# Self edges as a copied half tile, two extra gathers per half block, one weight table per block

## The chip, the cores and the metric

The kernel runs on one core of a Trainium2 chip. The metric is the device time of one execution in microseconds; the times shown are medians over runs. A profile is one execution recorded by the hardware, with its own time.

## The reference

A graph of 3327 nodes (padded to 3328 = 26 x 128) with 128 features, and a dense 3327 x 3327 matrix of edge weights in which about 2% of the entries are not zero; the diagonal always has its edge (the self edge). Two layers run one after the other:

```python
# layer 0: four heads of graph attention
h  = relu(layernorm(x))
x1, x2 = h @ w1[k], h @ w2[k]                        # per head k
s  = leaky_relu(x1[:, None] + x2[None, :], 0.01) @ a[k]
s  = exp(8 * tanh(s / 8)) * adj                      # zero where there is no edge
out_k = leaky_relu((s / s.sum(-1)) @ h @ Wlin[k].T, 0.01)
x  = x + concat(out_k) @ w
# layer 1: graph convolution with symmetric normalisation
h  = relu(layernorm(x)); A = adj + I; d = A.sum(1) ** -0.5
x  = x + relu((d[:, None] * A * d[None, :]) @ (h @ W.T + b))
```

## The kernel before

**Sparse scores.** A score is needed only where there is an edge. The kernel goes through the 26 blocks of 128 destination rows, each in two halves of 64 rows. It makes a list of the edges of each row and gathers, by indirect DMA, one table row per edge: 128 edges (one per partition) per gather. A table row holds the neighbour's normalised features (128), four score terms, ones, its x2 of all four heads (512), and in front of these (FEAT = 64 columns) the edge weights between this neighbour and the 64 rows of the half. There are two tables in HBM, one for each half; their weight columns are written anew by `weights` (L569 to L574) for every block and half, from AT_d, the transposed adjacency that `tables_step` (L352 to L362) writes.

**Lists.** `prep` (from L345) is a generator whose steps are dealt out among the other work. VectorE (DVE) turns the adjacency rows of a block into codes (L402), takes the largest eight codes of each short segment (L406), then selects, for each half of the columns, 32 entries per row by four rounds of "largest eight, remove them" over 136 candidates (L433 to L438), and 40 more from all 272 (the loop at L456 to L462). The first 64 fill a regular pattern of slots: 32 gathers per half, in four tiles `g` of eight gathers. What is left over, the extras, is packed by a small matrix product into OVT = 3 gathers per half, the tile `ge`. The self edge is an edge like any other in this list.

**Per half.** `groups` are nine steps m: two for each tile g and one, m = 8, for ge. `stage_z` (L577 to L603) turns the gathered x2 of four times 128 edges and four heads into PSUM by transposing on TensorE (L588). For g tiles DVE takes the maximum with -x1, which is laid out by slots (L600); for ge, x1 is added by a product with the incidence matrix `oi` (L591), and ScalarE (ACT) takes the relu (L597). `stage_r` (L605 to L612) multiplies with the attention vector: `sel` places the result of head h in rows of 32h to 32h + 31, four heads side by side in TensorE (L611). `finish` (from L615) turns the scores, takes tanh and exp, multiplies with the edge weights and aggregates (L659 for g, L677 for ge). `close` ends a half and, after the second, the block.

**Order and queues.** The order of instructions is written out by hand: `slot` is called several times per group and runs the pending ends, `advance` (which runs as many steps of `prep` of the next blocks as the time that has passed asks for), `fetch` (which queues the gathers of a tile as soon as its buffer is free: four buffers g, one ge) and `trickle` (which issues them). Gathers are issued by GpSimd (POOL); loads of the adjacency, weights, xn_d and hTb by SyncE (SP); AT_d by ACT. Each queue is in order.

**End.** Layer 1 is a matrix product over the transposed adjacency, read back from AT_d in strips of four blocks: a part in advance during the last block (`begin`, L874), the rest at the end (`layer1`, L938). `columns` (L831 to L841) cuts these reads.

Of the kernel before, what the change touches and what calls it, by code (L numbers as in the profile page):

```python
# [63 lines left out]
ROW = 720  # L64
COLS = 709
WIDE = 712
FEAT = 64
PROJ = 197
# [161 lines left out]
def _sparse_layers(tc, nc, x, adj, w1, w2, a, wlin, w, gw, gb, gb_sb, gwT, x_sb, dinv, flag, ident, out):  # L230
# [24 lines left out]
    with ExitStack() as l0:  # L255
        res = l0.enter_context(tc.tile_pool(name="res", bufs=1))
        dram = l0.enter_context(tc.tile_pool(name="dram", bufs=1, space=bass.MemoryType.DRAM))
        tables = [dram.tile([NP + 1, ROW], F32, name=f"table{k}") for k in range(2)]
# [5 lines left out]
        AT_d = dram.tile([NS * NP, 4 * P], F32, name="AT_d")  # L264
# [3 lines left out]
        sel = res.tile([P, H, 63], F32, name="sel")  # L268
        p_all = res.tile([P, NB, 2 * H], F32, name="p_all")
        code = res.tile([P, NP], mybir.dt.uint16, name="code")  # L270
        epos = res.tile([P, 2 * OVT], F32, name="epos")
# [10 lines left out]
        pat = l0.enter_context(tc.tile_pool(name="pat", bufs=4))  # L282
# [12 lines left out]
        nc.gpsimd.iota(epos, [[-P, 2 * OVT]], base=2 * NP, channel_multiplier=-1, allow_small_or_imprecise_dtypes=True)  # L295

        nc.gpsimd.iota(first, [[0, 2], [16, 4], [0, 2]], base=0, channel_multiplier=0, allow_small_or_imprecise_dtypes=True)
# [4 lines left out]
        nc.vector.tensor_scalar(hoff[:, :1], rowid, float(HALF), float(OVT * P), op0=OP.is_ge, op1=OP.mult)  # L302
        nc.vector.tensor_scalar(hoff[:, 1:], hoff[:, :1], float(OVT * P), None, op0=OP.add)
        nc.vector.tensor_scalar(rowid, hoff[:, :1], -HALF / (OVT * P), rowid, op0=OP.mult, op1=OP.add)
# [10 lines left out]
        nc.gpsimd.affine_select(lower[:, HALF:], lower[:, HALF:], [[0, HALF]], OP.is_ge, 0.0, base=-HALF, channel_multiplier=1)  # L315

# [28 lines left out]
        def prep(b, k):  # L345

            adjb = blks[b].adjb
            csum = pb.tile([P, 4], F32, name="csum")
# [3 lines left out]
            def tables_step(j0):  # L352
                n = min(4, NB - j0)
                pt = ps_tr.tile([P, 4, P], F32, name="tr")
                for q in range(n):
# [3 lines left out]
                at0 = (b // 4) * NP  # L359
                eng = nc.scalar if b else nc.sync  # L360
                eng.dma_start(AT_d[at0 + j0 * P:at0 + (j0 + n) * P, b % 4 * P:b % 4 * P + P].rearrange("(b p) c -> p b c", p=P),
                                  at[:, :n, :])  # L362
# [34 lines left out]
            for sgm in range(64):  # L397
                if sgm % 32 == 0:
                    codes = pa.tile([P, 2, part], mybir.dt.uint16, name="codes")
                    for i in range(2):  # L400
                        c0 = (sgm // 16 + i) * part
                        nc.vector.scalar_tensor_tensor(codes[:, i], adjb[:, c0:c0 + part], 0.0, code[:, c0:c0 + part],  # L402
                                                       op0=OP.not_equal, op1=OP.mult, accum_out=csum[:, sgm // 16 + i:sgm // 16 + i + 1])
                        yield
# [25 lines left out]
            lists = pb.tile([P, 64 + 46], F32, name="lists")  # L430
            k.lists = lists
            for c in range(2):
                for r in range(SLOTS // 8):  # L433
                    top = lists[:, SLOTS * c + 8 * r:SLOTS * c + 8 * r + 8]
                    nc.vector.max(top, cand[:, c, :SOME])
                    yield
                    nc.vector.match_replace(out=cand[:, c, :SOME], in_to_replace=top, in_values=cand[:, c, :SOME], imm_value=0.0)
                    yield  # L438
# [16 lines left out]
            flat = cand[:, :, :SOME]  # L455
            for r in range(EXTRA // 8):  # L456
                top = lists[:, 64 + 8 * r:64 + 8 * r + 8]
                nc.vector.max(top, flat)
                yield
                if r < EXTRA // 8 - 1:  # L460
                    nc.vector.match_replace(out=flat, in_to_replace=top, in_values=flat, imm_value=0.0)
                yield  # L462
# [12 lines left out]
            nc.scalar.copy(ext[:, 42:42 + H], p_all[:, b, H:])  # L475
            yield
# [12 lines left out]
            nc.vector.tensor_reduce(miss, csum, AX.X, OP.add)  # L489
# [5 lines left out]
            oi = pb.tile([P, 2 * OVT * P], F32, name="oi")  # L495
            nc.vector.tensor_scalar(oi, code[:, :2 * OVT * P], ext[:, 40:41], None, op0=OP.is_le)
            yield
            nc.vector.scalar_tensor_tensor(oi, code[:, :2 * OVT * P], end, oi, op0=OP.is_gt, op1=OP.mult)
# [6 lines left out]
            for t in range(2 * OVT):  # L505
                nc.tensor.matmul(ex_ps[:, t, :], oi[:, t * P:(t + 1) * P], ext, start=True, stop=True)
# [4 lines left out]
            rel = pb.tile([P, 2 * OVT], F32, name="rel")  # L511
            nc.vector.tensor_sub(rel, epos, ex[:, :, 40])
            big = [P, 2 * OVT, EXTRA]
            hit = pb.tile(big, F32, name="lq", bufs=1)
            nc.vector.tensor_tensor(hit, rel[:, :, None].to_broadcast(big), code[:, None, :EXTRA].to_broadcast(big), OP.is_equal)
            yield
            nc.vector.tensor_mul(hit, hit, ex[:, :, :EXTRA])
            hits = pb.tile([P, 2 * OVT], F32, name="hits")
            nc.vector.tensor_reduce(hits, hit, AX.X, OP.add)
            idxo = pb.tile([P, 2, OVT], mybir.dt.int32, name="idxo")  # L520
            nc.vector.tensor_scalar(idxo.rearrange("p c t -> p (c t)"), hits, -float(ROW), float(NP * ROW), op0=OP.mult, op1=OP.add)
# [30 lines left out]
        def gather(b, hb, w):  # L552

            k = blks[b]
            tab = tables[hb].rearrange("r (c u) -> (r c) u", u=1)
            if w == NW:
                g, n, at = pe_.tile([P, OVT, WIDE], F32, name="ge"), OVT, k.idxo[:, hb]
# [47 lines left out]
        def stage_r(k, hb, m, rs):  # L605
            n = 4 * P if m < 8 else OVT * P
            at = m % 2
            if at == 0:
                k.s = ps_s.tile([P, BANK], F32, name="s")
# [698 lines left out]
```

## Time and profile before

| | us |
|---|---|
| median of 3 runs | 2529.61 (2529.4 to 2537.58) |
| span of the profiled execution | 2534.6 |
| TensorE busy (modelled) | 2282.7 (90%) |
| VectorE busy | 2030.0 (80%) |
| ScalarE busy | 705.3 (28%) |
| GpSimd busy | 1792.0 (71%) |

The profiled execution took 2534.6 us from its first to its last instruction, 5 us more than the median of the runs. Issuing a DMA doesn't count as busy on SP and ACT; on POOL an indirect DMA does[...]. The mean granted TensorE clock is 0.979. The DMA engines are shown at 9 tenths or more in all slices but the last. A group's line reads: source line, engine, operation, output<-inputs by the program's names, shapes, count | busy us, mean ns of one | idle time of the engine before it, and who ended it.

### The profile page before, as it was taken

The page shows a single profiled execution, that of the slowest core. Times are in us where ns is not written, and L with a number is a line of the kernel's source. Part 1 is how long each engine was busy: PE and PEld are TensorE (multiplying, and loading weights), DVE is VectorE, ACT ScalarE, POOL GpSimd, SP SyncE. Part 2 cuts the span into 40 slices and gives each one's busy share as a digit, 9 for nine tenths or more (in the row PEclk, how much of TensorE's full clock was granted, in tenths as well). Part 3 has the DMA queues.
Part 4 walks back from the last instruction along what each step waited for, and adds up shares of the span by engine and source line. Part 5 has one row for each costly group of instructions (what it writes and reads, how often), then busy time and mean ns, then how long its engine had stood idle before and what let it go on. Part 6 is the DMA issues. An engine that isn't in the chain of part 4 may idle for free.

```text
span 2534.6 us, 51985 instructions
## 1 busy us (share of the span) xinstructions
PE 2282.7 (90%) x19410; PEld 1590.3 (63%) x19410; DVE 2030.0 (80%) x6260; ACT 705.3 (28%) x1651; POOL 1792.0 (71%) x1873
## 2 busy tenths in 40 slices
PE   6689999989988998999999999999999899999898
PEld 3466666666666666666666666666666666675553
DVE  7588988788887888888889888987988888795443
ACT  4122233223223222322322332232232223222110
POOL 3577777777777777777777777777777777777620
PEclk9699999999999999999999999999999999999999
DMA  9999999999999999999999999999999999999995
GB/s 298 389 333 334 332 357 317 329 352 334 315 338 343 319 327 358 324 328 344 339 316 340 355 314 338 348 334 321 343 344 317 324 361 314 332 323 343 328 333 196
DMA packets 460758, 838.58 MB, mean 331 GB/s; under 512 B 209098, under 2 KB 318164, under 8 KB 457172
## 3 DMA queue, kind: packets, MB, share of 16 engines
q0 software_dynamic: 145600, 640.34, 71.1%
q1 hardware_dynamic: 219396, 140.96, 19.1%
q10 hardware_dynamic: 95504, 53.88, 6.9%
q8 instruction: 156, 2.56, 0.4%
q14 instruction: 102, 0.84, 0.1%
HBM read 765.93 MB, written 113.42 MB: 347 GB/s over the span
## 4 chain that ended last, share of the span: by engine, by line
PE 36%; DVE 22%; DMA 20%; POOL 12%; issue 8%; ACT 0%; SPq 0%; DVEq 0%; POOLq 0%; ACTq 0%
DMA g<-table,idx 12%; POOL g L563 11%; DVE r L600 10%; PE z L588 10%; PE s L611 6%; DMA ge<-table,idxo 3%; PE z L591 3%; DMA AT_d<-at 2%; PE z L938 2%; DVE cand L406 2%; PE tr L628 2%; PE ag L659 2%; PE tr L371 1%; POOL ge L563 1%; DVE codes L402 1%
## 5 line engine op out<-in xcount | busy, mean ns | idle before, releaser
L563 POOL DMA_INDIRECT g<-table,idx x1664 | 1613.9, 970 | 568.4 <-issue 450.7
L588 PE MATMUL z<-ident,g 128*128 128x128 f32 x6656 | 929.9, 279 | 143.5 <-DVE r L600 106.2
L600 DVE TENSOR_TENSOR r<-z,x1n 128x1024 f32<-128x1024 f32 x832 | 1009.4, 1215 | 55.8 <-PE z L588 54.0
L588 PEld LDWEIGHTS z<-ident,g 128*128 128x128 f32 x6656 | 748.7, 142 | 361.7 <-DVE r L600 219.6
L611 PE MATMUL s<-r,sel 128*32 128x512 f32 (+1 forms) x3744 | 491.8, 598 | 0.7 <-ACT ssb L619 0.7
L619 ACT COPY ssb<-s 128x512 f32<-128x512 f32 x260 | 147.0, 565 | 533.9 <-PE s L611 531.4
L631 DVE TENSOR_TENSOR sc<-tr,g 128x32 f32<-128x32 f32 x208 | 38.4, 185 | 303.4 <-PE tr L628 303.4
L406 DVE MAX8 cand<-codes 128x8 f32<-128x52 uint16 x1664 | 214.9, 203 | 0.0
L563 POOL DMA_INDIRECT ge<-table,idxo x156 | 155.2, 995 | 49.0 <-issue 33.5
L639 ACT ACTIVATE th<-sc 128x32 f32<-128x32 f32 x260 | 58.3, 224 | 418.4 <-DVE sc L634 417.7
L591 PE MATMUL z<-oi,x1b 128*128 128x384 f32 x416 | 172.2, 496 | 0.0
L659 PEld LDWEIGHTS ag<-g,wt 128*32 128x32 f32 x3328 | 99.4, 110 | 115.4 <-issue 101.7
L358 ACT COPY at<-tr 128x512 f32<-128x512 f32 (+1 forms) x175 | 97.2, 555 | 215.9 <-PE tr L356 206.3
L628 PE MATMUL tr<-ident,ssb 128*128 128x128 f32 x988 | 152.6, 275 | 3.0 <-ACT at L358 2.7
L611 PEld LDWEIGHTS s<-r,sel 128*32 128x32 f32 x3744 | 73.9, 108 | 110.8 <-issue 86.6
L588 PEld LDWEIGHTS z<-ident,ge 128*128 128x128 f32 x624 | 80.7, 145 | 97.0 <-issue 27.7
L597 ACT ACTIVATE r<-z 128x768 f32<-128x768 f32 x104 | 84.4, 811 | 200.4 <-PE z L591 200.4
L659 PE MATMUL ag<-g,wt 128*32 128x133 f32 x3328 | 134.0, 279 | 0.0
L588 PE MATMUL z<-ident,ge 128*128 128x128 f32 x624 | 111.5, 282 | 23.3 <-DMA ge<-table,idxo 20.0
L356 PE MATMUL tr<-ident,adjb 128*128 128x128 f32 x676 | 107.8, 282 | 22.6 <-DMA adjb<-in_adj_dram 13.5
L628 PEld LDWEIGHTS tr<-ident,ssb 128*128 128x128 f32 x988 | 114.8, 141 | 11.1 <-ACT ssb L619 7.9
L402 DVE SCALAR_TENSOR_TENSOR codes<-adjb,code 128x832 uint16<-128x832 f32 x104 | 102.2, 1019 | 12.6 <-DMA adjb<-in_adj_dram 12.6
(188 smaller groups left out, 2347.4 us busy)
## 6 DMA issues: line engine op xcount, KB each, us to landing
adjb<-in_adj_dram SPq DMA_DIRECT2D x26, 1664.0 KB, 9.8
table<-AT_d SPq DMA_DIRECT2D x52, 832.0 KB, 17.0
AT_d<-at ACTq DMA_DIRECT2D x150, 256.0 KB, 5.7
g<-table,idx POOLq DMA_INDIRECT x1664
table<-img SPq DMA_DIRECT2D x12, 1312.0 KB, 4.9
adjb<-AT_d SPq DMA_DIRECT2D x18, 512.0 KB
g<-AT_d SPq DMA_DIRECT2D x7, 1024.0 KB
g<-AT_d ACTq DMA_DIRECT2D x5, 1024.0 KB, 11.0
```

What stands on the lines that cost most here:

```text
L356: nc.tensor.transpose(pt[:, q, :], adjb[:, (j0 + q) * P:(j0 + q + 1) * P], ident)
L358: nc.scalar.copy(at[:, :n, :], pt[:, :n, :])
L402: nc.vector.scalar_tensor_tensor(codes[:, i], adjb[:, c0:c0 + part], 0.0, code[:, c0:c0 + part], op0=OP.not_equal, op1=OP.mult, accum_out= ...
L406: nc.vector.max(cand[:, c, 8:].rearrange("p (r s) -> p r s", s=32)[:, :, sgm % 32], codes.rearrange("p a b -> p (a b)")[:, sgm % 32 * SEG: ...
L563: return nc.gpsimd.indirect_dma_start(out=g[:, t, lo:COLS], out_offset=None, in_=tab, in_offset=bass.IndirectOffsetOnAxis(ap=at[:, t:t + 1 ...
L588: nc.tensor.matmul(z[:, i, q * P:(q + 1) * P], g[:, m % 2 * 4 + q, PROJ + h * D:PROJ + (h + 1) * D], ident, is_transpose=True, start=(q == ...
L591: nc.tensor.matmul(z[:, i, :n], k.x1b[:, h * D:(h + 1) * D], k.oi[:, hb * n:(hb + 1) * n], start=False, stop=True, skip_group_check=True)
L600: nc.vector.tensor_tensor(r.rearrange("p h (i s) -> p h i s", s=16), z.rearrange("p h (i s) -> p h i s", s=16), k.x1n[:, 2 * hp:2 * hp + 2 ...
L611: nc.tensor.matmul(k.s[32 * h:32 * h + 32, :n], sel[:, h, 31 - at:63 - at], rs[h // 2][:, h % 2, :n], start=(at == 0), stop=(at == 1 or m ...
L619: nc.scalar.copy(ssb[:, :nk * P], s[:, :nk * P])
L628: nc.tensor.transpose(pt[:, q, :], ssb[:, q * P:(q + 1) * P], ident)
L659: nc.tensor.matmul(ag[32 * cg:32 * cg + 32, u, :WORK], wt[:, t].rearrange("p h q -> p (h q)"), g[:, t, FEAT:FEAT + WORK], start=(w == 0 an ...
```

## The change

Six things go together:

- The self edge is taken out of the codes: after L402, two DVE operations with the identity subtract the diagonal's code, and its sum is kept for the check that no edge is lost.
- The tile ge gets its self edges as a third, half-filled tile: 64 rows of the table copied by SP (the half's own rows, 64 partitions), beside FOUND = 2 gathered tiles instead of OVT = 3. ge becomes one lasting tile. For these 64 columns x1 comes by the maximum with x1n on DVE instead of the product with oi, which shrinks to two tiles; transposes and aggregation of this tile use 64 rows.
- Selection: all eight rounds of the first 64 entries go over both column halves' candidates (272) instead of four rounds for each (136).
- The table: rows are [64 weights | 648 body | 64 weights], 776 columns instead of 720; the second half's weights stand behind the body. The two tables alternate by blocks instead of by halves, and `weights` writes both halves' 128 columns at once, for the next block. A gather of the first half reads weights and body, one of the second body and weights.
- AT_d is laid out by blocks instead of by strips of four blocks. A strip is read back in one DMA for each block of it, in pieces of 128 columns instead of 512.
- The score matmul takes 2 columns of sel for each head instead of 32, into one lasting PSUM tile set to zero once; buffers `at` go from 4 to 3.

```diff
-ROW = 720
-COLS = 709
+FOUND = 2
+FEAT = 64
+BODY = 648
+ROW = FEAT + BODY + FEAT
+PROJ = 133
+COLS = 645
...
-        pat = l0.enter_context(tc.tile_pool(name="pat", bufs=4))
+        pat = l0.enter_context(tc.tile_pool(name="pat", bufs=3))
...
+                        lo, hi = max(c0, b * P), min(c0 + part, (b + 1) * P)
+                        if lo < hi:
+                            diag = pb.tile([P, P], F32, name="lq", bufs=1)[:, :hi - lo]
+                            mine = codes[:, i, lo - c0:hi - c0]
+                            nc.vector.scalar_tensor_tensor(diag, mine, -1.0, ident[:, lo - b * P:hi - b * P], op0=OP.mult, op1=OP.mult,
+                                                           accum_out=csum[:, sums[0]:sums[0] + 1])
+                            nc.vector.tensor_tensor(mine, mine, diag, OP.add)
+                            sums[0] += 1
...
-            for c in range(2):
-                for r in range(SLOTS // 8):
-                    top = lists[:, SLOTS * c + 8 * r:SLOTS * c + 8 * r + 8]
-                    nc.vector.max(top, cand[:, c, :SOME])
-                    yield
-                    nc.vector.match_replace(out=cand[:, c, :SOME], in_to_replace=top, in_values=cand[:, c, :SOME], imm_value=0.0)
-                    yield
+            flat = cand[:, :, :SOME]
+            def select(r):
+                top = lists[:, 8 * r:8 * r + 8]
+                nc.vector.max(top, flat)
+                yield
+                if 8 * r + 8 < 2 * SLOTS + EXTRA:
+                    nc.vector.match_replace(out=flat, in_to_replace=top, in_values=flat, imm_value=0.0)
+                yield
+            for r in range(SLOTS // 4):
+                yield from select(r)
...
-            tab = tables[hb].rearrange("r (c u) -> (r c) u", u=1)
+            tab = tables[b % 2].rearrange("(r u) -> r u", u=1)
             if w == NW:
-                g, n, at = pe_.tile([P, OVT, WIDE], F32, name="ge"), OVT, k.idxo[:, hb]
+                g, n, at = state["over"], FOUND, k.idxo[:, hb]
+                rows = b * P + HALF * hb
+                c0, n0 = (0, FEAT + COLS) if hb == 0 else (FEAT, BODY + FEAT)
+                nc.sync.dma_start(g[:HALF, FOUND, :n0], tables[b % 2][:NP * ROW].rearrange("(r c) -> r c", c=ROW)[rows:rows + HALF, c0:c0 + n0])
...
-        def weights(b, hb):
+        def weights(b):
-            c0 = b % 4 * P + HALF * hb
-            nc.sync.dma_start(tables[hb][:NP, :HALF].rearrange("(p r) c -> p r c", p=P),
-                              AT_d[b // 4 * NP:(b // 4 + 1) * NP, c0:c0 + HALF].rearrange("(p r) c -> p r c", p=P))
+            tab, of = tables[b % 2], AT_d[b * TURN:(b + 1) * TURN]
+            nc.sync.dma_start(tab[FEAT + BODY:FEAT + BODY + NP * ROW].rearrange("(p r c) -> p r c", p=P, c=ROW)[:, :, :2 * FEAT],
+                              of[FEAT:].rearrange("(p r c) -> p r c", p=P, c=P))
+            nc.sync.dma_start(tab[:FEAT].rearrange("(p c) -> p c", p=16), of[:FEAT].rearrange("(p c) -> p c", p=16))
...
                     if m == 8:
+                        nc.tensor.matmul(z[:, i, n:n + HALF], g[:HALF, FOUND, c0:c0 + D], ident[:HALF, :HALF],
+                                         is_transpose=True, start=False, stop=False, skip_group_check=True)
                         nc.tensor.matmul(z[:, i, :n], k.x1b[:, h * D:(h + 1) * D], k.oi[:, hb * n:(hb + 1) * n],
                                          start=False, stop=True, skip_group_check=True)
...
                 if m == 8:
                     nc.scalar.activation(r[:, :, :n], z[:, :, :n], AF.Relu)
+                    nc.vector.tensor_tensor(r[:, :, n:n + HALF], z[:, :, n:n + HALF],
+                                            k.x1n[:, 2 * hp:2 * hp + 2, HALF * hb:HALF * hb + HALF], OP.max)
...
-                nc.tensor.matmul(k.s[32 * h:32 * h + 32, :n], sel[:, h, 31 - at:63 - at], rs[h // 2][:, h % 2, :n],
+                nc.tensor.matmul(k.s[32 * h:32 * h + 2, :n], sel[:, h, 31 - at:33 - at], rs[h // 2][:, h % 2, :n],
...
+                    own = slice(0, P if t < FOUND else HALF)
+                    nc.tensor.matmul(ag[:, u, :WORK], wo[own, t, 4 * u:4 * u + 4].rearrange("p g h q -> p (g h q)"),
+                                     g[own, t, f0:f0 + WORK], start=False, stop=(t == OVT - 1), skip_group_check=True)
...
-                    if w == LATE and b + hb > 0 and b + hb < NB:
-                        queue.append((None, 0, 0, partial(weights, b + hb, 1 - hb)))
+                    if w == LATE and hb == (b == 0) and b + 1 < NB:
+                        queue.append((None, 0, 0, partial(weights, b + 1)))
...
-                w = min(4, NB - 4 * s) * P
-                yield v[:, at:at + n, :w], AT_d[s * NP + j * P:s * NP + (j + n) * P, :w].rearrange("(j p) i -> p j i", p=P)
+                for b in range(4 * s, min(4 * s + 4, NB)):
+                    a0 = b * TURN + j * P * P
+                    c0 = (b - 4 * s) * P
+                    yield v[:, at:at + n, c0:c0 + P], AT_d[a0:a0 + n * P * P].rearrange("(j p i) -> p j i", p=P, i=P)
```

## The prediction

> **What bounds the kernel now.** I read the page's costliest groups first, then everything about the gathers, then the busy time inside one block, then the rows that the change touches.
>
> The page: GpSimd (POOL) issues every gather, and memory is near its own limit.
>
> ```profile
> L563 POOL DMA_INDIRECT g<-table,idx x1664 | 1613.9, 970 | 568.4 <-issue 450.7
> ...
> L563 POOL DMA_INDIRECT ge<-table,idxo x156 | 155.2, 995 | 49.0 <-issue 33.5
> ...
> HBM read 765.93 MB, written 113.42 MB: 347 GB/s over the span
> ```
>
> "issue" is 450.7 us over 1464 gaps in the view of waits, 0.30 us each: POOL's own distance between two gathers. The view of that source line (minimum/median/maximum, then who waits):
>
> ```profile
> L563 POOL DMA_INDIRECT g<-table,idx x1664: 940/946/1773, 66.5 to 2424.1; - x185
> ...
> who waited for it (us, times):
>   PEld z L588: 58.5, 76
>   PE z L588: 41.8, 57
>   POOL g L563: 15.7, 43
> ```
>
> One gather costs 0.946 + 0.30 = 1.246 us of POOL whatever it moves. A block has 70 (64 for g, 6 for ge): 87.2 us. In the timeline of POOL, block 1's first gather is at 173.4 us and block 25's at 2331.0: 2157.6/24 = 89.9 us per block. The missing 2.7 us are gathers longer than 946 ns (mean 970 and 995: 1.8 us) and a few waits. So POOL issues without a pause for 24 blocks, and sets the pace.
>
> But nothing else is far behind. TensorE waits for gathers only 41.8/26 = 1.6 us per block (weight loads 58.5/26 = 2.2, mostly the same moments). The busy time inside block 11, cut where TensorE starts each gathered tile of the block (four g, then ge, for each half):
>
> ```profile
> 1095.30:1104.60 9.30, 7.62 (x69) 5.54 (x65) 9.03 (x25) 1.14 (x4) 7.10 (x8) 1.00 0.94 334
> ...
> 1114.40:1126.10 11.70, 10.84 (x94) 7.55 (x95) 11.25 (x31) 2.69 (x8) 8.88 (x10) 1.00 0.90 269
> 1126.10:1131.70 5.60, 5.60 (x48) 3.37 (x46) 0.63 (x4) 2.73 (x5) 4.15 (x5) 1.00 1.16 323
> ...
> 1152.70:1162.00 9.30, 8.12 (x81) 5.57 (x77) 9.23 (x42) 5.97 (x10) 7.17 (x8) 1.00 1.04 362
> 1162.00:1169.70 7.70, 6.96 (x68) 4.63 (x68) 7.53 (x21) 1.05 (x3) 5.88 (x7) 1.00 0.98 378
> ```
>
> After the length come PE, weight loads, DVE, ACT and POOL. In four of these stretches VectorE (DVE) is 96 to 99% busy; in the ge stretch (third line) TensorE is 100% busy and DVE idle. Without any wait for a gather this pair would need 89.9 less 1.6 to 2.2: 87.7 to 88.3 us per block. I take 87.9. POOL is the bound by 2 us per block; behind it stand DVE and TensorE by turns.
>
> **The change, part by part.**
>
> *One ge gather fewer per half.* 68 x 1.246 = 84.7, plus the same 2.7: **87.4 us** for POOL, 2.5 less. The copied rows go by SP (52 copies of 64 rows, 9.5 MB). SP waits there for the readers of ge in the half before, as POOL's ge gathers do; behind it in SP's queue stand the xn store, hTb and the next adjb, all wanted tens of us later. Cost 0; if a copy came after its two gathers, TensorE would wait for it in the ge stretch, some us per half.
>
> *Weight tables.* Two writes of 832 KB per block become one of 1664 KB, in half the packets at twice the size. SP issues it in the first half for the next block. Landing is now 17.0 us; twice that would still be a half early. It also drops a wait of POOL at every second half. Bytes: g about the same, ge 56.6 to 37.8 MB, copies +9.5: -11.5 MB.
>
> Here stands a rule of the Trainium skill ("DMA: Bandwidth & Descriptors", Specifications): about 358 GB/s of HBM per core. The row says 347, 97% of it. By the rule bytes decide: 879.4 to 867.9 MB, -1.3%, -33 us. By the rows they don't: POOL rarely waits for a landing (15.7 us in all), so the transfers keep up with its pace. I use POOL's rows and keep the rule as a rival.
>
> *DVE.* The rows:
>
> ```profile
> L435 DVE MAX8 lists<-cand 128x8 f32<-128x136 f32 x208 | 61.4, 295 | 1.3
> ...
> L437 DVE MATCH_REPLACE8 cand<-lists,cand 128x136 f32<-128x136 f32 x208 | 59.0, 284 | 0.0
> L458 DVE MAX8 lists<-cand 128x8 f32<-128x272 f32 x130 | 57.3, 441 | 2.7
> ...
> L461 DVE MATCH_REPLACE8 cand<-lists,cand 128x272 f32<-128x272 f32 x104 | 44.3, 426 | 0.0
> ...
> L377 DVE TENSOR_TENSOR part<-part,tr 128x128 f32<-128x128 f32 x50 | 13.7, 273 | 0.4 <-PE tr L371 0.4
> ```
>
> Selection: eight rounds per block over 272 candidates instead of 136: 8 x (441 - 295 + 426 - 284 - 12 for the value load, 92 to 80) = +2.2 us. Taking the diagonal out of the codes: 28 pieces in 26 blocks of two operations about 128 wide plus an accumulator read, 0.28 + 0.08 (rows of L725) + 0.27 (L377): +0.7. The max with x1, four of 128 elements from PSUM like L377: +1.1. Back: oi at two thirds (680 and 1006 ns): -0.55; three hit operations (about 405 ns) at two thirds of their length: -0.25; idxo twice: +0.2. Sum +3.4 us per block, 88 us in all.
>
> On the path only where DVE is full. The rounds run (block 11's: 1075.5 to 1085.3 us) over the end of a stretch like the last one above and then the ge stretch, where DVE has room; some 4.7 of the 8 rounds fall in the full one: +1.3. The diagonal falls into full stretches, +0.6; oi and hit come off one (11.25 of 11.70), -0.6. The max falls where DVE is idle: 0. Together **+1.3**; the ends are -0.6 (selection and diagonal hidden) and +3.4 (nothing hidden).
>
> *TensorE.* In the chain a head of the ge group is 0.33 us of transposes (three) and 0.65 of oi product (384 columns). After: 0.22 + half tile + 0.43. The half tile has 64 rows. The skill ("TensorEngine Tiling (Array Packing)", Key Properties) says that changing the tiling mode drains TensorE, which speaks against this part: two changes per head, and two more in the aggregation. It gives no price. The trace does: the score group L611, in 32-column mode, takes 0.99 to 1.00 us in the chain where L527, 512 columns in full mode, takes 0.86: 0.14 per pair of changes. Half tile 0.11 + 0.14: a head goes from 0.98 to 0.90, four -0.3; scores at 320 columns -0.1; aggregation +0.1. Per half -0.3, per block **-0.6**; without the drain -2.0, with twice its price +0.7. By the rule alone (a drain that eats the gain) it is 0. The relu's 811 ns become about 590 with the 0.27 of the max beside it: 0. Scores still go four heads at once; only the 30 idle columns of sel go.
>
> *The rest.* at buffers 4 to 3: a write lands 5.7 us after its issue, three steps are about 8 us apart: 0, at worst +10 in all. Start: block 0's lists come 2.2 + 0.7 later and the first gather waits for them: +3. Tail: AT_d by blocks makes the read-back of strips 512 B pieces where it was 2 KB, four times the issues. By the queue table ACT's queue (mostly such pieces) moves 53.88 MB in 6.9% of 16 engines, 308 GB/s; the gathers 355. 28 MB: 12 us more of transfer, 19 MB of it feeding layer 1, where TensorE is nearly full (95.27 of 96 us from 2400 on): 0 to +12, I take +5.
>
> **Sum.** TensorE and DVE: 87.9 + 1.3 - 0.6 = 88.6 us per block; POOL 87.4. The slower sets it: -1.3 x 24 = -31, blocks 0 and 25 -2, start +3, tail +5: **-25 us** on the profiled 2534.6, 2509.6. The median of the runs is 5 us below that execution, so **2505 us**.
>
> **Rivals.**
> (a) POOL alone decides: the additions find room. -2.5 x 24 = -60, blocks 0 and 25 -3, start and tail +8: 2475. For it: DVE is idle for 14 us of block 11 (76.2 busy of the 90.6 us in all ten stretches); against: not where the rounds fall.
> (b) Slower: DVE takes the bound. If all 3.4 us land on the path and the mode changes eat TensorE's gain, a block takes 87.9 + 3.4 = 91.3: +1.4 x 24 = +34, and +8: 2571. It decides once the added path exceeds 2.0 us per block. For it: four stretches at 96 to 99%.
> (c) Memory bound: -33 and +8: 2505, by other means; DMA share near 1.00 speaks for it, the rare waits of POOL against.
> (d) It doesn't do what it says: gain and added work cancel (path +1.7 or so, tail at its +12): 2530.
>
> **How the numbers follow.** Forecast 0.33, (a) 0.22, (b) 0.20, (c) 0.10, (d) 0.15. A difference under 0.5% (13 us) is no change for this kernel. Faster: most of the forecast (0.27), (a), 0.09 of (c): 0.58. Slower: most of (b) and a third of (d): 0.22. Same: 0.20. Range: from 2466, just under (a), to 2556, inside (b); the forecast alone 2487 to 2523.
>
> **What would show it.** Right: first gathers of two blocks about 88.6 us apart; 104 ge gathers at 946 ns; more waits of POOL for TensorE's aggregation than now, fewer of TensorE for gathers; the selection rows at 441 and 426; DVE near 2118 us. Wrong: blocks at 87.4 with POOL unbroken (a); blocks over 90 with DVE full and POOL waiting for buffers (b); TensorE waiting at the ge group for the copied rows; score groups over 1.1 us; strips that TensorE waits for at the end.

## The result: 0.7% slower

The changed kernel takes 2549.46 us (median of 5 runs, 2546.44 to 2557.68), the kernel before 2529.61 us (5 runs, 2526.45 to 2537.58). The ratio is 1.0073, with a 95% interval of 1.0052 to 1.0093. The forecast was 2505 us. The profiled execution of the changed kernel took 2547.16 us with a span of 2545.5 us; before, the span was 2534.6 us. The two spans are only 10.9 us apart where the medians are 19.9 us apart: the profiled execution before lies above the median of its kernel, the one after a little below. Executions of one kernel differ by some us, so a difference of 0.2 us per block between two profiles says little.

First the page of the changed kernel, the same rows as before:

```profile
HBM read 754.47 MB, written 113.22 MB: 341 GB/s over the span
...
L596 POOL DMA_INDIRECT g<-table,idx x1664 | 1615.3, 971 | 628.7 <-issue 407.2
...
L452 DVE MAX8 lists<-cand 128x8 f32<-128x272 f32 x338 | 147.8, 437 | 3.3
L635 DVE TENSOR_TENSOR r<-z,x1n 128x128 f32<-128x128 f32 x104 | 30.1, 289 | 140.3 <-ACT r L634 140.3
...
L455 DVE MATCH_REPLACE8 cand<-lists,cand 128x272 f32<-128x272 f32 x312 | 132.7, 425 | 0.0
...
L596 POOL DMA_INDIRECT ge<-table,idxo x104 | 98.6, 948 | 32.2 <-issue 17.7
```

There are 104 gathers into ge instead of 156, at 948 ns each, and the bytes fell from 879.4 to 867.7 MB. The selection rows are wide, at 437 and 425 ns. All of this is as expected. But POOL's idle time before its g gathers rose from 568.4 to 628.7 us. The view of the gathers' source line says why (minimum/median/maximum in ns first, then what POOL waited for, then who waited for a gather):

```profile
L596 POOL DMA_INDIRECT g<-table,idx x1664: 940/946/1783, 67.3 to 2415.5; - x185
...
  PE ag L701: 99.4, 65
...
who waited for it (us, times):
  POOL g L596: 22.4, 63
  PEld z L623: 6.7, 6
  PE z L623: 5.2, 3
```

TensorE's matmuls waited 41.8 us for gathers before, now 5.2. POOL in turn now waits 99.4 us for TensorE's aggregation to give buffers back. POOL stopped being the bound. Yet the pace did not change. TensorE's first transpose of a block (L588 before, L623 after) comes every 89.73 us before and every 89.70 us after, from block 1 to block 25. The busy time inside block 11, cut as before, shows what holds it (start and end, length, then the busy time of PE, weight loads, DVE, ACT and POOL, each with its number of instructions in brackets; at the end the granted clock, the busy share of the DMA engines and GB/s):

```profile
1100.90:1110.60 9.70, 7.97 (x69) 5.58 (x65) 9.39 (x26) 1.40 (x5) 7.27 (x9) 1.00 1.02 362
...
1120.10:1131.30 11.20, 10.74 (x94) 7.44 (x95) 10.75 (x32) 2.71 (x8) 8.46 (x10) 1.00 0.89 283
1131.30:1137.20 5.90, 5.90 (x49) 3.54 (x47) 1.27 (x6) 2.35 (x5) 4.38 (x6) 1.00 0.90 283
...
1158.70:1168.10 9.40, 8.02 (x77) 5.45 (x77) 9.33 (x43) 5.97 (x10) 5.93 (x7) 1.00 1.05 347
1168.10:1177.00 8.90, 7.17 (x69) 4.59 (x69) 8.73 (x21) 1.05 (x3) 6.77 (x8) 1.00 1.01 402
```

The ge stretch (third line) was 5.60 us and is 5.90, with TensorE busy all through. The last line was 7.70 us and is 8.90, with DVE busy for 8.73 of it; this is the largest growth. The first line grew too, from 9.30 to 9.70 us, with DVE busy for 9.39 of it. The second line, where DVE has less to do than before, went from 11.70 to 11.20. The last ge stretch of the block, where TensorE used to wait for gathers, got shorter (7.50 to 5.70 us).

Where the 10.9 us between the two spans are, by TensorE's transposes:

| part | before | after | difference |
|---|---|---|---|
| start to block 1 | 191.9 | 195.8 | +4.0 |
| 24 blocks | 2153.6 | 2152.9 | -0.7 |
| block 25, first to last transpose | 101.2 | 92.4 | -8.9 |
| last transpose to the end | 87.9 | 104.4 | +16.4 |

So there are two questions: why 24 blocks gained nothing, and why the end got longer.

### The profile page after: what moved, and what is told of

The parts are those of the page before. It is cut to its first block, busy times and chain, and to the rows that moved or that the text cites. A ratio compares the mean times of both kernels' runs of the same rounds, so it can differ in the third digit from the quotient of the medians.

```text
span 2545.5 us, 52430 instructions
## 1 busy us (share of the span) xinstructions
PE 2292.6 (90%) x19410; PEld 1580.1 (62%) x19410; DVE 2120.1 (83%) x6478; ACT 686.8 (27%) x1703; POOL 1737.1 (68%) x1822
## 4 chain that ended last, share of the span: by engine, by line
PE 39%; DVE 32%; DMA 16%; issue 6%; POOL 6%; ACT 0%; SPq 0%; DVEq 0%; ACTq 0%; POOLq 0%
DVE r L639 15%; DMA g<-table,idx 11%; PE z L623 11%; PE s L652 6%; POOL g L596 6%; PE z L628 5%; DVE cand L422 4%; DVE cand L455 2%; DVE lists L452 2%; PE ag L701 2%; PE tr L670 2%; DVE codes L410 2%; PE z L626 2%; PE z L984 1%; DMA g<-AT_d 1%
## 5 line engine op out<-in xcount | busy, mean ns | idle before, releaser
L596 POOL DMA_INDIRECT g<-table,idx x1664 | 1615.3, 971 | 628.7 <-issue 407.2
L623 PE MATMUL z<-ident,g 128*128 128x128 f32 x6656 | 922.2, 279 | 144.7 <-DVE r L639 129.6
L623 PEld LDWEIGHTS z<-ident,g 128*128 128x128 f32 x6656 | 745.9, 142 | 356.0 <-DVE r L639 253.5
L652 PE MATMUL s<-r,sel 128*2 128x512 f32 (+1 forms) x3744 | 475.3, 580 | 2.6 <-DVE s L649 1.9
L452 DVE MAX8 lists<-cand 128x8 f32<-128x272 f32 x338 | 147.8, 437 | 3.3
L635 DVE TENSOR_TENSOR r<-z,x1n 128x128 f32<-128x128 f32 x104 | 30.1, 289 | 140.3 <-ACT r L634 140.3
L628 PE MATMUL z<-oi,x1b 128*128 128x256 f32 x416 | 145.4, 431 | 0.0
L455 DVE MATCH_REPLACE8 cand<-lists,cand 128x272 f32<-128x272 f32 x312 | 132.7, 425 | 0.0
L365 PE MATMUL tr<-ident,adjb 128*128 128x128 f32 x676 | 108.9, 284 | 25.3 <-DMA adjb<-in_adj_dram 16.4
L596 POOL DMA_INDIRECT ge<-table,idxo x104 | 98.6, 948 | 32.2 <-issue 17.7
L652 PEld LDWEIGHTS s<-r,sel 128*2 128x2 f32 x3744 | 49.8, 82 | 101.8 <-issue 93.5
L634 ACT ACTIVATE r<-z 128x512 f32<-128x512 f32 x104 | 62.1, 597 | 187.0 <-PE z L628 186.9
```

Of the source, the lines that this page charges most:

```text
L596: return nc.gpsimd.indirect_dma_start(out=g[:, t, lo:hi], out_offset=None, in_=tab, in_offset=bass.IndirectOffsetOnAxis(ap=at[:, t:t + 1], ...
L623: nc.tensor.matmul(z[:, i, q * P:(q + 1) * P], g[:, m % 2 * 4 + q, c0:c0 + D], ident, is_transpose=True, start=(q == 0 or m < 8), stop=(m ...
L628: nc.tensor.matmul(z[:, i, :n], k.x1b[:, h * D:(h + 1) * D], k.oi[:, hb * n:(hb + 1) * n], start=False, stop=True, skip_group_check=True)
L652: nc.tensor.matmul(k.s[32 * h:32 * h + 2, :n], sel[:, h, 31 - at:33 - at], rs[h // 2][:, h % 2, :n], start=(at == 0), stop=(at == 1 or m = ...
```

## The experiments

The theory going in was this. In the blocks, the work added to TensorE and DVE used up the time that the gathers gave back; the largest part of it is the price of the half tile's mode changes. At the end, four times as many strip reads stand in ScalarE's queue ahead of its arithmetic. A mode change is TensorE's step from matmuls that use all its rows and columns to matmuls over 64 rows, or in a quarter of the columns as the scores are, or back. The rivals were memory as the bound, POOL never having been the bound, and a wrong idea of the pace without gather waits. "Per block" below is always the distance of TensorE's first transposes, averaged over blocks 1 to 25 of the profiled execution.

**The gather alone (e4_gather).** The kernel before, with two ge gathers per half; the third tile stays zero, so its extras' features are missing from the result.

```diff
-                g, n, at = pe_.tile([P, OVT, WIDE], F32, name="ge"), OVT, k.idxo[:, hb]
+                if b + hb == 0:
+                    state["over"] = pe_.tile([P, OVT, WIDE], F32, name="ge")
+                    nc.vector.memset(state["over"][:, 2:], 0.0)
+                g, n, at = state["over"], 2, k.idxo[:, hb]
```

> The kernel before with two instead of three gathers into ge per half block; the third tile is a lasting tile of zeros, so the features of its extras are left out of the result while all other work of it is done. POOL has 2.5 us per block less and nothing is added anywhere. As predicted (the pair of TensorE and VectorE needs 87.9 us per block without waits for gathers): 2475 to 2490 us. If the pair's own pace is 89 us or more: 2505 to 2520 us. If POOL was not the bound at all: 2528 to 2532 us.

Measured: 2489.70 us, ratio to before 0.9823 (0.9792 to 0.9855), 87.99 us per block. Its matmuls wait 8.7 us in all for gathers, where the kernel before had 41.8. So this is close to the pace of TensorE and DVE on their own; 87.9 was taken. Where it came from shows in the last ge stretch of block 11. Busy times by stretch, before:

```profile
1169.70:1177.20 7.50, 5.92 (x44) 3.27 (x44) 4.05 (x15) 1.93 (x3) 5.67 (x7) 1.00 1.02 349
```

and with one gather fewer:

```profile
1149.50:1155.00 5.50, 5.49 (x44) 3.21 (x44) 4.03 (x15) 1.93 (x3) 3.67 (x5) 1.00 1.03 403
```

TensorE works 5.5 us instead of waiting in 7.5. The gather was worth 1.74 us per block. The changed kernel removes it as well, so what the change adds must take 89.70 - 87.99 = 1.71 us per block of the path. The two gathers of a block take their bytes along, 0.67 MB or 2.2%, so this run alone does not tell POOL from memory. POOL's own rows speak for POOL: before, it issued with hardly a pause. And over blocks 1 to 25 the kernel before moved 334 GB/s, this one 333, while f7_fullsel below reached 338. At that rate the bytes of the kernel before would let a block take 88.7 us, 1.0 less than it took.

**No mode changes (e2_full).** The changed kernel, with the copied rows taken as a whole tile whose lower 64 rows are zero. The result is the same.

```diff
-                        nc.tensor.matmul(z[:, i, n:n + HALF], g[:HALF, FOUND, c0:c0 + D], ident[:HALF, :HALF],
+                        nc.tensor.matmul(z[:, i, n:n + P], g[:, FOUND, c0:c0 + D], ident,
...
-                    own = slice(0, P if t < FOUND else HALF)
+                    own = slice(0, P)
```

> The changed kernel with the half tile of copied rows taken through TensorE as a whole tile of 128 rows (rows 64 to 127 hold zeros): transposes of 128 rows, scores unchanged, aggregation over 128 rows. No change of TensorE's tiling mode is left between the transposes and the oi product of a head or in the aggregation of ge. Theory A (two mode changes per head cost about 0.29 us instead of the 0.14 taken, and TensorE sets the pace in the ge stretch): a head goes from 1.05 to about 0.76 us, eight heads and the aggregation give 2 to 2.7 us per block, of which 1.5 to 2.4 arrive: 2494 to 2515 us. Theory B (VectorE or memory sets the pace of the block): TensorE's ge stretch gets shorter and the next stretch longer, 2540 to 2552 us.

Measured: 2502.83 us, ratio to before 0.9882 (0.9853 to 0.9912), 1.9% under the changed kernel; 88.06 us per block, 1.64 less. More work on TensorE, and less time. TensorE's timeline shows one head after the other (start, length of the group, line, shapes; the modelled lengths overlap, so read the starts). The changed kernel:

```profile
1132.34 0.38 PE L623 MATMUL z<-ident,ge 128*128 128x128 f32 x2
1132.65 0.27 PE L626 MATMUL z<-ident,ge 64*128 64x64 f32 x1
1132.85 0.70 PE L628 MATMUL z<-oi,x1b 128*128 128x256 f32 x2
1133.38 0.38 PE L623 MATMUL z<-ident,ge 128*128 128x128 f32 x2
```

With the whole tile:

```profile
1111.41 0.38 PE L623 MATMUL z<-ident,ge 128*128 128x128 f32 x2
1111.62 0.27 PE L626 MATMUL z<-ident,ge 128*128 128x128 f32 x1
1111.73 0.60 PE L628 MATMUL z<-oi,x1b 128*128 128x256 f32 x2
1112.17 0.38 PE L623 MATMUL z<-ident,ge 128*128 128x128 f32 x2
```

The half tile starts 0.31 us after the first of the two transposes instead of 0.21. The product starts 0.20 after the half tile instead of 0.11, and the next head 0.53 after the product instead of 0.44. Each of the three steps loses about 0.1 us. The third lies inside the product, which the profile shows as two matmuls: the second starts 0.320 us after the first instead of 0.218, and from there to the next head it is 0.216 in both. TensorE's weight loads (PEld) show what is lost. The changed kernel:

```profile
1132.64 0.13 PEld L626 LDWEIGHTS z<-ident,ge 64*128 64x128 f32 x1 [0.17 <-issue]
1132.85 0.30 PEld L628 LDWEIGHTS z<-oi,x1b 128*128 128x128 f32 x2
```

With the whole tile:

```profile
1111.52 0.14 PEld L626 LDWEIGHTS z<-ident,ge 128*128 128x128 f32 x1
1111.63 0.30 PEld L628 LDWEIGHTS z<-oi,x1b 128*128 128x128 f32 x2
```

With the whole tile a load starts about 0.11 us ahead of its matmul (1111.52 for 1111.62, 1111.63 for 1111.73), that is together with the matmul before. In the changed kernel the load of the half tile and the first load of the product start together with their own matmul (1132.64 for 1132.65). So it is in all 208 heads: the median lead of these two loads is 0.002 us, against 0.108 with the whole tile. The loads that otherwise run behind the matmul before stand on the path.

The median steps of a head, over all blocks, add up to 0.975 us before, 1.049 in the changed kernel and 0.761 with the whole tile. From the first aggregation product of a ge group to the next matmul it is 1.362, 1.651 and 1.362 us. The half tile so costs TensorE 8 x 0.288 + 2 x 0.289 = 2.9 us per block over a whole one; 1.64 of it arrive in the pace.

**The selection (e3_sel).** The changed kernel with the 64 slots chosen as before, four rounds over each half's 136 candidates. At most three extras of a row are counted and the test for missed edges is left out, so the result lacks edges.

```diff
             def select(r):
                 top = lists[:, 8 * r:8 * r + 8]
-                nc.vector.max(top, flat)
+                of = cand[:, r // 4, :SOME] if r < SLOTS // 4 else flat
+                nc.vector.max(top, of)
```

> The changed kernel with the 64 slots chosen as before the change: four rounds over each half's 136 candidates instead of eight over 272. To keep the extra rows within two tiles per half block, at most three extras of a row are counted and the test for a missed edge is left out, so some edges are left out of the result; all other instructions stay. VectorE has 2.2 us less per block. Theory A (the rounds that fall into the full stretch arrive on the path, +1.08 us measured in the fourth window of the second half): 1.0 to 1.4 us per block less, 2515 to 2526 us. Theory B (VectorE is not what holds the pace; TensorE is): 2542 to 2552 us.

Measured: 2518.36 us, ratio to before 0.9941 (0.9925 to 0.9958); 88.74 us per block, 0.97 less. The stretch of block 11 that had grown to 8.90 us, in the busy times by stretch of this kernel:

```profile
1161.00:1168.70 7.70, 6.92 (x68) 4.51 (x68) 7.53 (x21) 1.05 (x3) 5.87 (x7) 1.00 0.99 373
```

It is back at the 7.70 us of before, with DVE at 7.53 as before. Not all of the 0.97 need be the selection: what the run leaves out besides (the addition of the missed-edge flag, 159 ns, and a shorter count of the extras) is 0.20 us of DVE per block. The start comes back too: block 0's first transpose is at 75.6 us before, 79.9 in the changed kernel and 75.8 here.

**The diagonal and the maximum (g9_nodiag, g8_nomax).** The first leaves out the two operations that take the diagonal out of the codes (with the same cut of the extras; self edges then count twice). The second takes the half tile through the relu with the rest, so the self edges' scores lack x1.

```diff
-                        if lo < hi:
+                        if False:
```

```diff
-                    nc.scalar.activation(r[:, :, :n], z[:, :, :n], AF.Relu)
-                    nc.vector.tensor_tensor(r[:, :, n:n + HALF], z[:, :, n:n + HALF],
-                                            k.x1n[:, 2 * hp:2 * hp + 2, HALF * hb:HALF * hb + HALF], OP.max)
+                    nc.scalar.activation(r[:, :, :n + HALF], z[:, :, :n + HALF], AF.Relu)
```

> The changed kernel without taking the diagonal out of the codes (28 pieces in 26 blocks, 0.7 us of VectorE per block); at most three extras of a row are counted and the test for a missed edge is left out, so some edges are left out of the result and the self edges are in it twice. As predicted (they fall into full stretches and 0.6 us per block arrive): 14 us less, 2533 to 2540 us. Rival (hidden): 2544 to 2555 us.

> The changed kernel without VectorE's maximum over the half tile: ScalarE's relu runs over all 320 columns instead of 256, so x1 is left out of the scores of the self edges. VectorE has 1.1 us per block less and no longer waits for ScalarE's relu (140 us in all, 5.4 us per block, in the profile of the changed kernel). As predicted (the maximum falls where VectorE is idle and costs nothing): within 6 us of the changed kernel, 2544 to 2555 us. Rival (VectorE, held in its queue behind the relu, starts the selection rounds later): 0.4 us per block or more, 2540 us or less.

Measured: without the diagonal step 2531.07 us, ratio to before 0.9991 (0.9977 to 1.0005), 89.02 us per block, 0.68 less. DVE is busy 0.80 us less per block here, of which again 0.20 are the flag and the count, so the diagonal step itself may be worth a little less. Without the maximum 2550.00 us, 1.0054 (1.0035 to 1.0072), 89.80 us per block: no difference from the changed kernel. The 140.3 us that DVE waits for ScalarE's relu ahead of the maximum cost nothing that shows; DVE has room there (1.27 us busy in the ge stretch of 5.90).

**The strips (e1_strips, f6_sp).** The first puts the transposed adjacency back into strips of 512 columns. The second keeps the new layout and only lets SyncE issue every strip read.

```diff
-                at0 = b * TURN + j0 * P * P
-                eng.dma_start(AT_d[at0:at0 + n * P * P].rearrange("(b p c) -> p b c", p=P, c=P), at[:, :n, :])
+                at0 = (b // 4) * NP
+                eng.dma_start(AT_d[at0 + j0 * P:at0 + (j0 + n) * P, b % 4 * P:b % 4 * P + P].rearrange("(b p) c -> p b c", p=P),
+                                  at[:, :n, :])
...
-                for b in range(4 * s, min(4 * s + 4, NB)):
-                    a0 = b * TURN + j * P * P
-                    c0 = (b - 4 * s) * P
-                    yield v[:, at:at + n, c0:c0 + P], AT_d[a0:a0 + n * P * P].rearrange("(j p i) -> p j i", p=P, i=P)
+                w = min(4, NB - 4 * s) * P
+                yield v[:, at:at + n, :w], AT_d[s * NP + j * P:s * NP + (j + n) * P, :w].rearrange("(j p) i -> p j i", p=P)
```

```diff
-                eng = nc.scalar if k % 2 else nc.sync
+                eng = nc.sync
```

> The changed kernel with the transposed adjacency stored in strips of 512 columns again, as before the change, so that layer 1 reads strips in rows of 2 KB with a quarter of the DMAs; the weight table of a block is then written by two DMAs of 256 B pieces instead of one of 512 B pieces. Everything else of the change stays. Theory A (the end is late because ScalarE and SyncE issue four times as many strip reads, 20.7 us of which stand ahead of the last half's close on ScalarE): the stretch from the last gather to the end goes from 126.5 back to about 106 us, the total to 2530 to 2538 us. Theory B (the reads are late because of the bytes per piece alone, hidden either way, and the end is late because POOL's last gathers are no longer what it waits for): within 4 us of 2549.

> The same kernel as in the run called e6_sp (all strip reads of the changed kernel issued by SyncE). Theory A (ScalarE is held by the issuing, so the last close comes late): 2534 to 2542 us, no wait of ScalarE for strip reads ahead of the close. Theory B (the reads in 512 B pieces are slow, or SyncE alone issues them too slowly): 2546 to 2560 us, TensorE waiting for strips.

(With strips of 512 columns the weight table of a block is written by two DMAs from the strip.) Measured: strips as before 2532.15 us, ratio to before 0.9997 (0.9986 to 1.0009), 0.8% under the changed kernel; SyncE alone 2543.22 us, 1.0039 (1.0025 to 1.0052). From the last transpose to the end it is 87.9 us before, 104.4 in the changed kernel, 98.8 with SyncE alone and 90.6 with the strips. ScalarE's timeline at the close of the last half (an entry with q is DMA issuing; the bracket is idle time before the instruction and what ended it), the changed kernel:

```profile
2454.99 19.57 ACTq L894 DMA_DIRECT2D g<-AT_d  x18
2474.61 0.63 ACT L736 ACTIVATE agn<-ag,rec 128x128 f32<-128x128 f32 x2 [20.74 <-DMA g<-AT_d]
```

With strips as before:

```profile
2460.14 4.77 ACTq L894 DMA_DIRECT2D g<-AT_d  x4
2464.96 0.62 ACT L738 ACTIVATE agn<-ag,rec 128x128 f32<-128x128 f32 x2 [12.35 <-DVE rec L733]
```

With SyncE issuing all:

```profile
2464.06 0.62 ACT L736 ACTIVATE agn<-ag,rec 128x128 f32<-128x128 f32 x2 [11.98 <-DVE rec L731]
```

Eighteen issues keep ScalarE for 19.57 us, and the normalisation of the last half (agn) starts only when they are out. TensorE waits for it; its timeline in the changed kernel:

```profile
2475.03 0.74 PE L742 MATMUL tr<-ident,agn 128*128 128x128 f32 x2 [9.62 <-ACT agn L736]
```

With ScalarE free, agn starts 10.6 us earlier, but SyncE then issues 48 reads in a row, and the reads that the next strip needs stand behind them. These lines are SyncE's, first in the changed kernel, where ScalarE issues its eighteen beside it, then with SyncE alone:

```profile
2454.94 28.52 SPq L894 DMA_DIRECT2D g<-AT_d  x24
```

```profile
2461.29 29.93 SPq L894 DMA_DIRECT2D g<-AT_d  x48
2491.32 0.78 SPq L939 DMA_DIRECT2D r<-xn_d  x1
```

While both engines issue, from 2454.94 to 2474.56, 35 reads go out (18 and 17), one in 0.56 us; SyncE alone takes 0.62. The second engine adds little. In the chain of work from 2430 us on, SyncE's issuing has 28.1% with SyncE alone, the strip reads' landings 21.8% and layer 1's products 13.8%; with strips of 512 columns the products have 48.2%, and strip reads are not among the larger shares. The total fell between the two forecasts. Moving the issues off ScalarE is worth 5.6 of the 13.8 us between 104.4 and 90.6, net of the longer queue on SyncE. The other 8.2 go with the number and the pieces of the reads, whoever issues them; these two were not told apart. The blocks took 90.08 us with the strips, in an execution that lies 6 us above the median of that kernel, so whether the table's 256 B pieces cost 0.4 us per block stays open.

**Two corrections at once (e5_both, f5_both) and two causes at once (e7_fullsel, f7_fullsel).** e5_both is e2_full with e1_strips; e7_fullsel is e2_full with e3_sel (and so lacks edges). They ran first together with SyncE issuing all (e6_sp), on a chip on which the kernel before itself took 3221.15 us.

> Both corrections in one: the changed kernel with the half tile taken as a whole tile of 128 rows (no changes of the tiling mode in the ge group) and with the transposed adjacency in strips of 512 columns as before the change. If the two causes are independent (mode changes in every block, strip reads at the end), the gains of the two add: 2549 - 47 - 17 = 2485, so 2480 to 2491 us. If the 256 B pieces of the weight table (0.38 us per block in the first of the two) weigh more once the blocks are shorter, or POOL becomes the bound: 2491 to 2500 us.

> The changed kernel with all strip reads issued by SyncE, none by ScalarE; the layout by blocks, the pieces of 512 B and the number of DMAs stay. Theory A (ScalarE is held by the issuing, so the last close comes late): ScalarE no longer waits ahead of the close, TensorE's 9.6 us wait for it goes, 2534 to 2542 us. Theory B (the reads as such are slow in 512 B pieces, or SyncE alone issues them too slowly): the close is early but TensorE waits for strips, 2546 to 2560 us.

> The changed kernel with the half tile as a whole tile of 128 rows and the 64 slots chosen in four rounds over each half's 136 candidates, both undone at once (at most three extras of a row are counted and the test for a missed edge is left out, so some edges are left out of the result). Each alone gave 1.64 and 0.97 us per block. If TensorE and VectorE each hold their own stretch, the two add: 89.7 - 2.6 = 87.1 us per block, which POOL's 68 x 1.246 + 2.7 = 87.4 would not let through entirely: 87.4 to 87.8, 2484 to 2496 us. If POOL already decides at the 88.06 of the whole tile alone: 88.0, 2498 to 2504 us.

Measured there: 3285.34 us (1.0189 of before), 3316.40 us (1.0278) and 3312.75 us (1.0277). Every forecast was missed. The page of e5_both:

```profile
HBM read 754.46 MB, written 113.20 MB: 264 GB/s over the span
...
PE 44%; DVE 22%; another core or an unknown queue 17%; issue 7%; ACT 5%; DMA 3%; POOL 1%; SPq 0%; ACTq 0%; DVEq 0%; POOLq 0%
...
L596 POOL DMA_INDIRECT g<-table,idx x1664 | 1607.7, 966 | 1324.4 <-PE ag L703 688.3
```

A gather takes 966 ns as elsewhere, but 17% of the chain of work is put to a queue that the profile doesn't know, and TensorE's granted clock is 0.907, against 0.979 for the same code on the other chip below. A block took 119 to 121 us. What held the engines stays open; with another bound, these runs say nothing on the causes here. The same three kernels ran again, on another chip, where before took 2532.81 us:

> The same kernel as in the run called e5_both (whole tile of 128 rows for the copied rows, strips of 512 columns as before the change), because in that call every kernel, the one before included, took 27% longer, with memory at 264 GB/s and TensorE held by waits that no kernel's own work explains. If the two causes are independent: 2485, so 2480 to 2491 us, 0.982 of before. If the 256 B pieces of the weight table weigh more once the blocks are shorter, or POOL becomes the bound: 2491 to 2500 us.

> The same kernel as in the run called e7_fullsel (whole tile of 128 rows and the slots chosen per half; at most three extras of a row counted and the test for a missed edge left out, so some edges are left out of the result). If TensorE and VectorE each hold their own stretch: 87.4 to 87.8 us per block, 2484 to 2496 us. If POOL already decides at the 88.06 of the whole tile alone: 88.0, 2498 to 2504 us.

Measured: both corrections 2486.30 us, ratio 0.9813 (0.9795 to 0.9831), 1.9% faster than before; the sum of the two single gains had given 2485. Whole tile and old selection 2481.70 us, 0.9794 (0.9772 to 0.9816), 87.23 us per block, a little under the expected floor of 87.4; the sum of the two single gains had given 87.1. POOL is again close to the bound there: TensorE's matmuls wait 35.8 us for gathers, against 5.2 in the changed kernel and 41.8 before, and POOL waits only 7.0 us for buffers of the aggregation instead of 99.4. TensorE and DVE each hold their own stretch, and the causes add.

## Why the prediction was wrong

*What bounds the kernel: right.* The gathers held the kernel before by 89.73 - 87.99 = 1.74 us per block (predicted 2.0), with TensorE and DVE right behind. For the changed kernel the rival by memory fell: it moves 1.3% fewer bytes than before and takes longer, and the whole tile, with the changed kernel's bytes, takes 1.9% less. For the kernel before it is weakened only: by the rates above, at least 1.0 of the 1.74 us is not memory's, if its smaller pieces of the weight tables move as fast.

*TensorE, -0.6 us per block: this step failed.* A head was to go from 0.98 to 0.90 us and went to 1.05; the term is +0.5 to +0.9 instead of -0.6. A pair of mode changes was priced at 0.14 us and costs 0.29, in a head as in the aggregation. The price was read from the length of a score group alone, from its first matmul to the one behind it. The step into the group is left out in this, and the record before shows it:

```profile
1127.40 0.81 PE L591 MATMUL z<-oi,x1b 128*128 128x384 f32 x2
1128.05 0.49 PE L588 MATMUL z<-ident,ge 128*128 128x128 f32 x3
...
1129.53 0.81 PE L591 MATMUL z<-oi,x1b 128*128 128x384 f32 x2
1130.27 1.07 PE L611 MATMUL s<-r,sel 128*32 128x512 f32 x8
```

From the product to the next head it is 0.65 us, from the same product to a score group 0.74. The same step from a transpose is 0.203 us instead of 0.109. With these 0.09 a pair has 0.23 us, and ten pairs per block (eight heads, two aggregations) turn -0.6 into +0.3. The remaining 0.05 per pair were not in the rows that were read.

Measured, the ge groups have 8 x 0.074 + 2 x 0.289 - 2 x 0.132 = +0.9 us per block; the last term is the scores over 320 columns, 0.783 to 0.651 us, about the 0.1 predicted. A term taken at nothing helped: a score group over 512 columns got 0.026 us shorter with 2 columns of sel instead of 32 (0.996 to 0.970), 16 times per block, -0.4. That leaves +0.5 for TensorE as a whole, but these groups lie largely where DVE sets the pace. The end named for twice the price was +0.7, so the range held it and the value chosen did not. The rule of the Trainium skill weighed there ("TensorEngine Tiling (Array Packing)", Key Properties: a change of tiling mode drains TensorE) was a better guide than the row: by the rule alone the step was 0, and the truth was on the far side of it. The weight loads above, which no longer run ahead of their matmul, fit the rule; that nothing else about the 64 rows adds to the cost is not shown.

*DVE, +3.4 us per block, +1.3 on the path: about right.* Busy DVE over blocks 3 to 22 went from 76.15 to 79.57 us per block, in all to 2120.1 us (2118 predicted). Of the selection up to 0.97 arrived (1.3 predicted), of the diagonal up to 0.68 (0.6), of the maximum nothing (0). The shorter oi and hit operations (-0.6) were not run alone.

*The sum per block.* Taking TensorE's +0.9 in full, 87.99 + 0.9 + 0.97 + 0.68 - 0.6 = 89.9, and up to 0.4 less without the flag and count that two of the runs left out besides; measured 89.70. The -0.6 is an estimate and the +0.9 need not arrive in full, so this agreement is good to a few tenths only. That gain and additions cancel to 0.03 us is chance. The prediction had 88.6. Its own threshold for the slower rival, 2.0 us of added path, was not reached; 1.71 is what the rival of cancelling work (d) had named. So -31 us for the 24 blocks became -0.7.

*Start, +3: right*; block 0's first transpose came 4.3 us later, and the old selection alone takes 4.1 of them back.

*Tail, +5 (0 to +12): too small, and by another mechanism.* It was reckoned from the rate of small pieces. From block 25's first transpose to the end, it is 181.5 us with strips as before and 196.7 in the changed kernel: +15.2. Part of that is no transfer at all but ScalarE's queue, where arithmetic stands behind DMA issues. A good part of it was hidden by block 25 itself, which got 8.9 us shorter (-2 was taken for blocks 0 and 25 together). The prediction did not look at what ScalarE still had to compute between its issues, nor at how long a quarter of a read takes to issue.

*Weight tables, row copies, at buffers: cost nothing visible in the blocks, as predicted.* In block 11 TensorE starts on ge without a gap, so the copied rows are there in time.

Together: +30 us in the blocks, +1 at the start, -7 in block 25 and +11 after it are the 36 us between the predicted 2509.6 and the span of 2545.5.

## What to carry to other kernels

A matmul over half the rows was no saving between full ones: filled up with zeros, the same tile was faster. Price a mode change by all the steps around it, the one into it included, up to the start of the next matmul; the length of the group in the other mode leaves some of them out. When an engine computes and issues DMAs, count its issues at the stage where its arithmetic sets the end, before cutting a transfer into more reads. And when two engines stand 2 us behind the bound, a gain is worth only what the additions to those two leave of it.

## What the runs showed of the hardware

- A 64-row transpose between 128-row matmuls delayed three starts, its own and the next two, by about 0.1 us each: 1.049 us per head against 0.761 with 128 rows. Two 64-row products behind four of 128 rows cost 0.289 us in the same way (1.651 against 1.362). In the heads, the weight loads of the half tile and of the product behind it start 0.002 us ahead of their matmul instead of 0.108.
- Eighteen strip reads issued back to back took ScalarE 19.57 us, 1.09 us each (up to 256 KB); four of up to 1 MB took 4.77, 1.19 each. There the time per read did not go with its size. SyncE alone issued 48 small ones in 29.93 us, 0.62 each; ScalarE and SyncE together issued 35 in 19.62 us, 0.56 per read.
- On one chip the four kernels that ran there took 27 to 33% longer than elsewhere, and the order of two of them was turned round (1.0189 of before against 0.9813 for the same code); the cause is not known.
